# Block sums of a message-passing layer as two 64-column products, and the general path in a branch of its own

## The chip, the cores and the metric

The kernel runs on one core of a Trainium2 chip. The metric is the device time of one execution in microseconds (us), read as the median of several runs. The engines are named as in the profile: PE (TensorE, matrix products), PEld (its weight loads), DVE (VectorE), ACT (ScalarE), POOL (GpSimd, which issues the gathers) and SP (SyncE, which issues plain DMAs).

## The reference

A PaiNN layer on a graph of 1250 nodes with 512 features and 40000 edges that are sorted by their end node `dst`, then a residual and a layer norm. Cut to what matters here:

```python
x_j = x[src]                                  # a gather: 40000 rows
s_j = silu(x_j[:, 384:] @ W1 + b1) @ W3 + b3
split = s_j * (rbf(r) * cutoff(r) @ W2 + b2)
v_msg = v_j * s1 + s3 * edge_attr             # 384 columns
x = x + segment_sum(concat([v_msg, s2]), dst) # first round of sums
row = node_update(x)                          # U, V, Wu1, Wu2: a row for each node
x = x + segment_sum(row[src], dst)            # second round of sums
out = layernorm(x0 + x)
```

## The kernel before, in words

**Tiling.** The sorted edges are cut into 79 chunks of 512 (`CHUNK`), the last of them not full. Four chunks make a group (`CPG`), so there are 20 groups (`NGR`), and two groups feed one block of 128 nodes, so there are 10 blocks (`NB`). The chunk with number c is expected to end in a window of 32 places (`WIN`) that begins 16c - 8 nodes in; neighbouring windows overlap by half, since a chunk's own share is 16 nodes (`SHARE`). If any edge lies outside its chunk's window, the count `misses_v` is not zero and the whole work is done by another function, `general`, in place of `windowed`. With these inputs the count is zero and `windowed` runs. The choice stands at L383 to L387 as an `If` with an `Else`.

**A step.** `windowed` walks over 80 batches t, four to a group; a batch is 4 tiles of 128 edges, one from each chunk of the group. A batch's work:
- `gather` (L745, POOL): four indirect DMAs bring the 128 rows of 640 values of each tile, three batches ahead.
- `edge_factors` (L854, PE): four products make `eb`, the factors of each edge, in four PSUM banks that exist once.
- `messages` (DVE): `hot` (L812, one-hot rows of the place in the window, 32 wide), two multiplications of the gathered rows by `eb` (L865, L869), `pair` (L883) and `spread` (L823). All of them read `eb` or come before the last one that does, so the next `edge_factors` waits for L869.
- `add_messages` (L900, L907, PE): products with `hot` and `spread` as weights of 32 columns add the messages into the PSUM tile `agg`. The four chunks of a group use the four quarters of `agg`: 128 rows, 32 for each chunk. `count_links` (L925) adds up in `adj` which sources each place has, for the second round. `agg` and `adj` exist once.

**Closing a group.** After a group's fourth batch `close_group` (L933 to L956, ACT) copies `agg` to SBUF and makes `high` (L949) and `both` (L951) of `adj`; DVE then does L960 with `both`. An even group goes whole, 128 rows, into the tile `sums_0`. An odd group goes with its first 112 rows (`KEPT`) into its tile `sums_1`, and its last 32 rows are copied once more, to the same rows of the tile of the next odd group (L956). Rows 112 to 127 of an odd group's tile so hold what the odd group before it found for places of this block, and its own last 16 rows stand in the next one's tile alone. Group 1's tile begins with zeros there.

**A block.** `sum_block` (L992, PE) adds the two groups of a block up: `sel` has two matrices of 128 x 128 with a one where a row of the tile belongs to a place of the block (L274), and two products with them add into one PSUM tile, first the even group's and then the odd's. `take_block` (DVE, L1008) adds the nodes' values. The block's node update follows in small pieces on all engines over the next ten steps, among them `turn_nodes` (L1031), `times_u` (L1042), its copy `vu` to SBUF (L1051, ACT) and `times_uv` (L1058, PE). These pieces share one PSUM bank, `work`, so `times_uv` waits until `vu` has been copied out. In the last blocks' steps PE also begins the second round of sums (L1248, `begun`).

**What orders the work.** The order is written out by hand (manual schedule): lists of tasks by step and rank, run at four places of a step. In each step DVE's messages are issued first, then the tasks of `first`, then `add_messages` and `count_links` of the batch before, the tasks of `early`, `edge_factors` of the next batch, a gather, the tasks of `late`, and those of `dve`. Each engine runs its own instructions in that order. Even groups close in step 8b + 4 and odd ones in step 8b + 8 (b from 0). The `vu` copy of the block before falls into the same step as the closing of an even group and stands behind it.

Of the kernel before, what the change touches and what calls it, by code (L numbers as in the profile page):

```python
# [11 lines left out]
F32 = mybir.dt.float32  # L12
# [5 lines left out]
ALU = mybir.AluOpType  # L18
# [3 lines left out]
P = 128  # L22
# [18 lines left out]
WIN = SHARE + 2 * MARGIN  # L41
GSPAN = CPG * SHARE
REACH = GSPAN - SHARE + WIN
KEPT = P - 2 * MARGIN
# [20 lines left out]
def gnn_resnorm(  # L65
# [31 lines left out]
    nc = tc.nc  # L97
    n_nodes, width = x.shape
# [4 lines left out]
    NGR = -(-NCH // CPG)  # L103
    NCP = NGR * CPG

    sh = Shared()
# [116 lines left out]
    for i in range(GROUP):  # L223
# [32 lines left out]
    place = front.tile([P, 3], F32)  # L256
# [7 lines left out]
        place[:, 0:1], place[:, 2:3], float(SHARE - WIN) / WIN, part, op0=ALU.mult, op1=ALU.add  # L264
    )
    nc.vector.tensor_scalar(
        place[:, 2:3], place[:, 0:1], float(P - GSPAN), float(-P), op0=ALU.is_ge, op1=ALU.mult
    )
    nc.vector.scalar_tensor_tensor(
        place[:, 1:2], place[:, 0:1], float(GSPAN), place[:, 2:3], op0=ALU.add, op1=ALU.add  # L270
    )
    sh.sel = const.tile([P, 2, P], F32, name="sel")
    for k in range(2):
        nc.vector.tensor_scalar(sh.sel[:, k, :], lane, place[:, k : k + 1], None, op0=ALU.is_equal)  # L274


    local_r = front.tile([NCP, CHUNK], F32)
# [103 lines left out]
    front_scope.close()  # L381

    misses_v = nc.values_load(missed_i[0:1, 0:1], min_val=0, max_val=n_edges)  # L383
    with tc.If(misses_v == 0) as in_windows:
        windowed(tc, sh)
    with in_windows.Else():
        general(tc, sh)  # L387


# [197 lines left out]
def windowed(tc, sh):  # L587
# [62 lines left out]
    with tc.tile_pool(name="msg", bufs=4) as pool, tc.tile_pool(  # L650
# [72 lines left out]
                nc.vector.memset(magic[:, k : k + 1], (MAGIC, -MAGIC)[k])  # L723


        sums = {1: pool.tile([P, width], F32, name="sums_1", bufs=2)}
        nc.gpsimd.memset(sums[1][P - WIN :, :], 0.0)

        def work():
            return ps_work.tile([P, BANK], F32, name="work")  # L730
# [201 lines left out]

        def close_group(g):  # L933
            agg, rows = aggs.pop(g), group_rows(g)
            if g % 2 == 0:
                assert rows == P
                sums[g] = pool.tile([P, width], F32, name="sums_0", bufs=1)
                nc.scalar.copy(sums[g], agg)
            else:
                if rows < KEPT:  # L940
                    assert rows == P - WIN
                    nc.vector.memset(sums[g][rows:KEPT, :], 0.0)
                own = min(rows, KEPT)
                nc.scalar.copy(sums[g][:own, :], agg[:own, :])
# [6 lines left out]
            nc.scalar.activation(both[:, 1], high, AF.Identity, bias=magic[:, 1:2])  # L951
            boths[g] = both
            if g % 2 and g + 2 < NGR:
                assert rows == P
                sums[g + 2] = pool.tile([P, width], F32, name="sums_1", bufs=2)
                nc.scalar.copy(sums[g + 2][P - WIN :, :], agg[P - WIN :, :])  # L956

        def low_counts(g):
            both = boths[g]
# [27 lines left out]
        def sum_block(b, k):  # L987
            if k == 0:
                blks[b] = (
                    work() if b < NB - 1 else ps_sum.tile([P, BANK], F32, name="begun")  # L990
                )
            nc.tensor.matmul(  # L992
                blks[b], sh.sel[:, k, :], sums.pop(2 * b + k), start=(k == 0), stop=(k == 1)
            )

        node_x = pool.tile([P, width], F32, name="node_x", bufs=1)
# [316 lines left out]
        def at(when, step, rank, fn, *args):  # L1313
            when.setdefault(step, []).append((rank, fn, args))
# [562 lines left out]
```

## Time and profile before

| What | Value |
|---|---|
| median of 3 runs | 594.64 us (591.26 to 596.64) |
| the profiled execution's own time | 585.79 us |
| its span, from the first to the last instruction | 583.8 us |
| granted clock of PE over the span | 0.888 |
| busy: PE / PEld / DVE / ACT / POOL | 445.5 / 240.2 / 441.8 / 373.6 / 354.5 us |
| DMA | 126.95 MB at 217 GB/s |

The profile is one execution. A row of the timeline gives a start in us, a length in us, the engine, the source line, the operation, what it writes and reads, the shapes, a count of merged instructions and, in brackets, how long the engine was idle before it and who ended that wait. A row of a group gives the busy time in us and the mean length in ns. A matmul in fp32 stands in the trace as two records. Ends of matmuls are modelled. "issue" is a wait for which the profile shows no cause.

### The profile page before, as it was taken

To read this page: it belongs to the slowest core of one execution; us is meant where nothing else is said; L and a number is where in the kernel's file an instruction comes from. 1 tells how busy PE (TensorE), PEld (TensorE's weight loads), DVE (VectorE), ACT (ScalarE), POOL (GpSimd) and SP (SyncE) were. 2 spreads that over 40 slices of the span, in tenths; PEclk is the share of its full clock that TensorE was granted. 3 is DMA by queue.
4 is the path that set the end of the run, shared out by engine and by line. 5 is a ranking of instruction groups with operands and counts; after the bars stand their busy time and mean duration, and the time that the engine had idled before them with its cause. 6 is when DMAs were issued, how large, how long until landed. Compare 5 with 4: busy or idle time off the path is not lost. (4 is left out here: it accounts for less than half of the span.)

```text
span 583.8 us, 11028 instructions
## 1 busy us (share of the span) xinstructions
PE 445.5 (76%) x4193; PEld 240.2 (41%) x4193; DVE 441.8 (76%) x698; ACT 373.6 (64%) x941; POOL 354.5 (61%) x369
## 2 busy tenths in 40 slices
PE   2845667687777887697888786787777878798894
PEld 1422323344444344334435443443443444353673
DVE  7685867878878777878877777777787777687685
ACT  1455364757677665767776767777667778656455
POOL 7265767656667665656656665666666576643850
PEclk9966986888899777979888889998989899889998
DMA  8766777786777767767877777777777787859514
GB/s 240 257 189 213 200 224 216 210 262 200 216 224 243 228 197 218 214 205 220 253 245 201 253 226 213 233 231 242 220 229 224 218 240 224 241 148 285 210 38 146
DMA packets 38321, 126.95 MB, mean 217 GB/s; under 512 B 6688, under 2 KB 8238, under 8 KB 38258
## 3 DMA queue, kind: packets, MB, share of 16 engines
q0 software_dynamic: 26016, 104.86, 60.5%
q1 hardware_dynamic: 10910, 20.64, 10.2%
q10 hardware_dynamic: 1332, 0.64, 0.4%
q8 instruction: 35, 0.57, 0.4%
q14 instruction: 28, 0.23, 0.1%
HBM read 114.78 MB, written 11.34 MB: 216 GB/s over the span
## 5 line engine op out<-in xcount | busy, mean ns | idle before, releaser
L745 POOL DMA_INDIRECT more<-table,src_i x189 | 189.9, 1005 | 107.3 <-issue 44.0
L745 POOL DMA_INDIRECT nodes<-table,src_i x124 | 126.3, 1019 | 74.0 <-issue 28.3
L854 PE MATMUL eb<-w_sb,basis_t 25*128 25x388 f32 x626 | 83.5, 585 | 76.6 <-issue 42.2
L845 ACT ACTIVATE one<-one,weight,src_f 128x128 f16<-128x128 f16 x313 | 128.5, 482 | 0.5 <-issue 0.2
L835 ACT ACTIVATE one<-number,low 128x128 f16<-128x128 f16 x313 | 99.8, 392 | 8.5 <-PE adj L925 3.3
L812 DVE TENSOR_TENSOR hot<-lane,eb 128x128 f32<-128x128 f32 (+1 forms) x81 | 22.7, 281 | 81.6 <-PE eb L854 44.7
L869 DVE TENSOR_TENSOR more<-more,eb 128x1536 f32<-128x1536 f32 (+2 forms) x49 | 82.6, 1688 | 0.0
L854 PEld LDWEIGHTS eb<-w_sb,basis_t 25*128 25x128 f32 x626 | 27.5, 196 | 99.5 <-issue 58.0
L900 PE MATMUL agg<-more,hot 128*32 128x512 f32 (+1 forms) x378 | 66.0, 752 | 1.2 <-ACT sums L956 1.2
L865 DVE TENSOR_TENSOR more<-more,eb 128x1024 f32<-128x1024 f32 (+2 forms) x49 | 57.5, 1175 | 0.4 <-issue 0.3
L907 PEld LDWEIGHTS agg<-more,spread 128*32 128x32 f32 x1134 | 39.5, 125 | 40.8 <-issue 40.1
L869 DVE TENSOR_TENSOR nodes<-nodes,eb 128x1536 f32<-128x1536 f32 (+1 forms) x32 | 54.2, 1695 | 0.0
L907 PE MATMUL agg<-more,spread 128*32 128x128 f32 x1134 | 47.8, 298 | 0.0
L823 DVE TENSOR_TENSOR spread<-hot,eb 128x384 f32<-128x384 f32 (+1 forms) x81 | 43.0, 532 | 0.0
L925 PE MATMUL adj<-pair,one 128*128 128x160 f16 x313 | 37.9, 243 | 5.0 <-issue 4.9
L900 PE MATMUL agg<-nodes,hot 128*32 128x512 f32 x248 | 38.5, 680 | 2.4 <-ACT sums L956 2.4
L883 DVE TENSOR_TENSOR pair<-number,column 128x640 f16<-128x640 f16 (+1 forms) x81 | 38.5, 476 | 0.0
L805 ACT COPY basis_t<-work 128x512 f32<-128x512 f32 x20 | 11.7, 587 | 41.1 <-PE work L800 21.7
L865 DVE TENSOR_TENSOR nodes<-nodes,eb 128x1024 f32<-128x1024 f32 (+1 forms) x32 | 37.8, 1180 | 0.0
L960 DVE SCALAR_TENSOR_TENSOR both<-both,adj 128x400 f16<-128x400 f16 (+1 forms) x20 | 11.3, 566 | 32.0 <-ACT both L951 21.1
L907 PEld LDWEIGHTS agg<-nodes,spread 128*32 128x32 f32 x744 | 23.6, 116 | 23.1 <-issue 22.9
L925 PEld LDWEIGHTS <-one 128*128 128x128 f16 x313 | 20.8, 100 | 22.1 <-issue 20.7
(258 smaller groups left out, 728.8 us busy)
## 6 DMA issues: line engine op xcount, KB each, us to landing
table<-more SPq DMA_DIRECT2D x10, 320.0 KB
spilled<-begun SPq DMA_DIRECT2D x12, 256.0 KB
more<-table,src_i POOLq DMA_INDIRECT x189
more<-spilled SPq DMA_DIRECT2D x2, 1280.0 KB
resid<-h_t SPq DMA_DIRECT2D x9, 256.0 KB
node_x<-in_x_dram SPq DMA_DIRECT2D x8, 256.0 KB
nodes<-table,src_i POOLq DMA_INDIRECT x124
nodes<-in_x_dram POOLq DMA_DIRECT2D x2, 768.0 KB
```

What stands on the lines that cost most here:

```text
L745: got = nc.gpsimd.indirect_dma_start(out=rows_t[:n, j, :], out_offset=None, in_=sh.table1, in_offset=bass.IndirectOffsetOnAxis(ap=sh.src_i ...
L812: nc.vector.tensor_tensor(hots[t][:m, js, :], lane[:m, None, :WIN].to_broadcast(shape), eb[:m, js, V + 3 : V + 4].to_broadcast(shape), op= ...
L823: nc.vector.tensor_mul(spread[t][:m, js], hots[t][:m, js, None, :].to_broadcast(shape), eb[:m, js, V : V + 3, None].to_broadcast(shape),)
L835: nc.scalar.activation(onehots[t][:, j, :], number[:, :P], AF.Abs, bias=low[:, e : e + 1])
L845: nc.scalar.activation(one, one, AF.Relu, scale=less[:, e : e + 1], bias=worth[:, e : e + 1])
L854: made = nc.tensor.matmul(eb[:, j, : V + CARRY], turned[g][rows, i, :], sh.w2_sb[rows, :], start=True, stop=True,)
L865: nc.vector.tensor_mul(msg[:m, js, V:], msg[:m, js, V:], eb[:m, js, C:V])
L869: nc.vector.tensor_mul(msg[:m, js, :V].rearrange("p t (k c) -> p t k c", k=3), msg[:m, js, :V].rearrange("p t (k c) -> p t k c", k=3), eb[ ...
L883: nc.vector.tensor_tensor(pair[:m, js, :].rearrange("p t (l h) -> p t l h", h=2), number[:m, : PARTS * WIN].rearrange("p (l h) -> p l h", ...
L900: nc.tensor.matmul(agg[j * WIN : (j + 1) * WIN, :], hots[t][:m, j, :], msg[:m, j, :width], start=(i == 0), stop=False, skip_group_check=True,)
L907: nc.tensor.matmul(agg[j * WIN : (j + 1) * WIN, c * C : (c + 1) * C], spread[t][:m, j, c, :], msg[:m, j, width:], start=False, stop=(i == ...
L925: nc.tensor.matmul(to[:, :, at : at + WIN], one[:m, j, :], pair[:m, j, :].rearrange("e (p n) -> e p n", n=WIN), start=(i == 0 and j == js[ ...
```

## The change

It has three parts.

1. **The groups' tiles.** Each group, even or odd, copies its first 112 rows into its own tile, and, after `high` and `both`, its last 32 rows into rows 96 to 127 of the tile of the *next* group (before: odd groups only, and into the tile of the next odd group). The pools for even groups' tiles hold two and for odd groups' tiles one (before: one and two). The zeros go to group 0's tile.
2. **The block's sums.** A group's tile now holds all that belongs to its own 64 places and nothing else. `sel` becomes one matrix of 128 x 64, the same for both groups. The two products write the upper and the lower 64 rows of the block's PSUM tile, each with `start` and `stop`, instead of adding into all 128. Both are listed as tasks of `first` in the step after the odd group's closing (before: the first of them in `late` of the closing step). For the last block the list is as before.
3. **The branches.** `general` stands in an `If` of its own with the opposite condition, in place of the `Else`.

```diff
-    sh.sel = const.tile([P, 2, P], F32, name="sel")
-    for k in range(2):
-        nc.vector.tensor_scalar(sh.sel[:, k, :], lane, place[:, k : k + 1], None, op0=ALU.is_equal)
+    sh.sel = const.tile([P, GSPAN], F32, name="sel")
+    nc.vector.tensor_scalar(sh.sel, lane[:, :GSPAN], place[:, 1:2], None, op0=ALU.is_equal)
...
-    with tc.If(misses_v == 0) as in_windows:
+    with tc.If(misses_v == 0):
         windowed(tc, sh)
-    with in_windows.Else():
+    with tc.If(misses_v != 0):
         general(tc, sh)
...
-        sums = {1: pool.tile([P, width], F32, name="sums_1", bufs=2)}
-        nc.gpsimd.memset(sums[1][P - WIN :, :], 0.0)
+        sums = {}
+
+        def room_for_sums(g):
+            sums[g] = pool.tile([P, width], F32, name=f"sums_{g % 2}", bufs=2 - g % 2)
+            return sums[g][P - WIN :, :]
+
+        nc.gpsimd.memset(room_for_sums(0), 0.0)
...
         def close_group(g):
             agg, rows = aggs.pop(g), group_rows(g)
-            if g % 2 == 0:
-                assert rows == P
-                sums[g] = pool.tile([P, width], F32, name="sums_0", bufs=1)
-                nc.scalar.copy(sums[g], agg)
-            else:
-                if rows < KEPT:
-                    assert rows == P - WIN
-                    nc.vector.memset(sums[g][rows:KEPT, :], 0.0)
-                own = min(rows, KEPT)
-                nc.scalar.copy(sums[g][:own, :], agg[:own, :])
+            if rows < KEPT:
+                assert rows == P - WIN and g == NGR - 1
+                nc.vector.memset(sums[g][rows:KEPT, :], 0.0)
+            own = min(rows, KEPT)
+            nc.scalar.copy(sums[g][:own, :], agg[:own, :])
...
-            if g % 2 and g + 2 < NGR:
+            if g + 1 < NGR:
                 assert rows == P
-                sums[g + 2] = pool.tile([P, width], F32, name="sums_1", bufs=2)
-                nc.scalar.copy(sums[g + 2][P - WIN :, :], agg[P - WIN :, :])
+                nc.scalar.copy(room_for_sums(g + 1), agg[P - WIN :, :])
...
             nc.tensor.matmul(
-                blks[b], sh.sel[:, k, :], sums.pop(2 * b + k), start=(k == 0), stop=(k == 1)
+                blks[b][k * GSPAN : (k + 1) * GSPAN, :], sh.sel, sums.pop(2 * b + k),
+                start=True, stop=True,
             )
...
-                at(late, begin, 1, sum_block, b, 0)
-                at(first, begin + 1, 1, sum_block, b, 1)
+                for k in range(2):
+                    at(first, begin + 1, 1, sum_block, b, k)
```

The order of the built programs shows where this lands. First ACT where group 2, an even one, is closed and block 0 is being updated. Before (`sums` with a number is one group's tile, `one` the sources' marks of `distances` and `mark_sources`):

```order
L835 ACTIVATE one<-number,low 128x128 x4
L938 COPY sums_1079<-agg 128x512
L949 ACTIVATE high<-adj,magic 128x400
L951 ACTIVATE both<-high,magic 128x400
L1051 COPY vu<-work 128x384
L845 ACTIVATE one<-one,weight,src_f 128x128 x4
```

The same place now:

```order
L837 ACTIVATE one<-number,low 128x128 x4
L941 COPY sums_867<-agg 112x512
L946 ACTIVATE high<-adj,magic 128x400
L948 ACTIVATE both<-high,magic 128x400
L952 COPY sums_1084<-agg 32x512
L1048 COPY vu<-work 128x384
L847 ACTIVATE one<-one,weight,src_f 128x128 x4
```

One copy of 32 rows stands between `both` and `vu` now; the first copy has 112 rows in place of 128. This happens at all ten even groups; odd groups have the same instructions as before.

Then PE at block 0's sums. Before:

```order
L925 MATMUL adj<-pair,one 128x5x32
L854 MATMUL eb<-w_sb,basis_t 128x388 x4
L992 MATMUL work<-sums_659,sel 128x512
L992 MATMUL work<-sums_340,sel 128x512
L900 MATMUL agg<-nodes,hot 32x512 x4
```

And now:

```order
L927 MATMUL adj<-pair,one 128x5x32
L856 MATMUL eb<-w_sb,basis_t 128x388 x4
L988 MATMUL work<-sums_339,sel 64x512
L988 MATMUL work<-sums_663,sel 64x512
L902 MATMUL agg<-nodes,hot 32x512 x4
```

The two products stand at the same place of PE's order as before, although their lines in the task lists differ; each has 64 rows of output.

Last POOL where `windowed` begins. Before, with `ISA` an instruction that adds to a gather queue's semaphore, one ahead of each of the first eight gathers (the first three are shown):

```order
L997 MEMSET node_x 128x512
L1873 ISA
L745 DMA more<-table_189,src_i 128x640
L1873 ISA
L745 DMA more<-table_189,src_i 128x640
L1873 ISA
```

And now:

```order
L786 MEMSET basis 128x16x12
L787 MEMSET basis 128x16
L994 MEMSET node_x 128x512
L747 DMA more<-table_188,src_i 128x640 x12
L747 DMA nodes<-table_188,src_i 128x640 x8
```

The eight stand elsewhere now: where `general` is passed over at the end there is one such instruction for all eight semaphores. Each engine there goes through a second comparison and three jumps (from the end of `windowed` over its own empty other side, over `general`, and to the end), where before it made one jump over `general`. SP's part of the passed-over side has eight more waits for semaphores.

More of the change, by code (lines that the diff above doesn't have):

```diff
@@ L266, in gnn_resnorm @@
     nc.vector.tensor_scalar(
-        place[:, 2:3], place[:, 0:1], float(P - GSPAN), float(-P), op0=ALU.is_ge, op1=ALU.mult
+        place[:, 2:3], place[:, 0:1], float(GSPAN), float(-GSPAN), op0=ALU.is_ge, op1=ALU.mult
     )
-    nc.vector.scalar_tensor_tensor(
-        place[:, 1:2], place[:, 0:1], float(GSPAN), place[:, 2:3], op0=ALU.add, op1=ALU.add
-    )
-    sh.sel = const.tile([P, 2, P], F32, name="sel")
-    for k in range(2):
-        nc.vector.tensor_scalar(sh.sel[:, k, :], lane, place[:, k : k + 1], None, op0=ALU.is_equal)
+    nc.vector.tensor_add(place[:, 1:2], place[:, 0:1], place[:, 2:3])
+    sh.sel = const.tile([P, GSPAN], F32, name="sel")
+    nc.vector.tensor_scalar(sh.sel, lane[:, :GSPAN], place[:, 1:2], None, op0=ALU.is_equal)
     local_r = front.tile([NCP, CHUNK], F32)
```

## The prediction

> **What bounds the kernel now.** The chain at the page's end covers only the last 32 us, so I read the page's busy times first, then who waits for whom, and then the timeline of single steps, since the kernel is 80 steps of the same form.
>
> ```profile
> PE 445.5 (76%) x4193; PEld 240.2 (41%) x4193; DVE 441.8 (76%) x698; ACT 373.6 (64%) x941; POOL 354.5 (61%) x369
> ...
> L812 DVE TENSOR_TENSOR hot<-lane,eb 128x128 f32<-128x128 f32 (+1 forms) x81 | 22.7, 281 | 81.6 <-PE eb L854 44.7
> ```
>
> No engine is full. DVE is idle 81.6 us in front of `hot`, the first instruction of a step, about 1.0 us a step, and mostly for PE's `eb`. One ordinary step from the timeline shows why:
>
> ```profile
> 163.57 1.74 DVE L869 TENSOR_TENSOR nodes<-nodes,eb 128x1536 f32<-128x1536 f32 x1
> 165.37 0.93 PE L854 MATMUL eb<-w_sb,basis_t 25*128 25x388 f32 x8 [0.49 <-issue]
> 167.49 0.29 DVE L812 TENSOR_TENSOR hot<-lane,eb 128x128 f32<-128x128 f32 x1 [1.57 <-PE eb L854]
> ```
>
> L869 ends at 165.31, PE begins `eb` 0.06 us later, and `hot` comes at 167.49, 2.18 us after L869. That is a loop through DVE and PE: messages, then `eb`, then messages. PE work costs nothing as long as `eb` can begin right behind L869. The gathers are not in the loop: `hot` waits for PE and not for a DMA. So every edit is priced at the two steps in which a group closes, where ACT comes into the loop.
>
> **Part 1: two products of 64 columns.** By form, the lines of the group view:
>
> ```profile
> L900 PE MATMUL agg<-more,hot 128*32 128x512 f32 x376 | 65.0, 753 | 1.2 <-ACT sums L956 1.2
> ...
> L992 PE MATMUL work<-sums,sel 128*128 128x512 f32 x36 | 24.2, 802 | 0.6 <-ACT sums L944 0.6
> ...
> L956 ACT COPY sums<-agg 32x512 f32<-32x512 f32 x9 | 5.2, 577 | 0.2
> ```
>
> The products with 32 columns run beside each other: 376 records of 753 ns are 283 us in 65.0 us of busy time, 4.4 at once. L992, with 128 columns, has 36 records of 802 ns in 24.2 us, 1.2 at once. So two products of 64 columns should take about half of 24.2 us over nine blocks, 12.1 us less of PE. Whether a step gets shorter depends on what follows. The step in which group 5 closes:
>
> ```profile
> 197.02 1.99 PE L992 MATMUL work<-sums,sel 128*128 128x512 f32 x4
> 197.03 0.58 ACT L944 COPY sums<-agg 112x512 f32<-112x512 f32 x1 [3.33 <-PE adj L925]
> 198.38 0.63 ACT L951 ACTIVATE both<-high,magic 128x400 f16<-128x400 f32 x1
> 199.03 0.58 ACT L956 COPY sums<-agg 32x512 f32<-32x512 f32 x1
> 199.04 0.57 DVE L960 SCALAR_TENSOR_TENSOR both<-both,adj 128x400 f16<-128x400 f16 x1 [2.80 <-ACT both L951]
> 199.53 0.28 DVE L812 TENSOR_TENSOR hot<-lane,eb 128x128 f32<-128x128 f32 x1
> 199.66 1.06 PE L900 MATMUL agg<-nodes,hot 128*32 128x512 f32 x8 [0.66 <-ACT sums L956]
> 201.72 1.74 DVE L869 TENSOR_TENSOR more<-more,eb 128x1536 f32<-128x1536 f32 x1
> 203.52 0.93 PE L854 MATMUL eb<-w_sb,basis_t 25*128 25x388 f32 x8 [1.76 <-issue]
> ```
>
> DVE waits 2.80 us for ACT's chain copy, `high`, `both`, and goes on to `hot` without a wait for PE. PE ends the two products at 199.01 and then waits 0.66 us until ACT has emptied `agg`. Ending them a microsecond earlier only makes that wait longer; then PE is idle 1.76 us more before `eb`, which begins when L869 is done (203.46). So here the gain is zero. It isn't where PE runs at half of its clock; the block with the longest products:
>
> ```profile
> 249.25 3.78 PE L992 MATMUL work<-sums,sel 128*128 128x512 f32 x4
> ...
> 252.18 1.75 DVE L869 TENSOR_TENSOR nodes<-nodes,eb 128x1536 f32<-128x1536 f32 x1
> ...
> 255.71 0.93 PE L854 MATMUL eb<-w_sb,basis_t 25*128 25x388 f32 x8
> 256.71 0.29 DVE L812 TENSOR_TENSOR hot<-lane,eb 128x128 f32<-128x128 f32 x1 [1.54 <-PE eb L854]
> ```
>
> L869 ends at 253.93, so `hot` could come at 256.11 (2.18 us later, as above) and comes at 256.71. Half of 3.78 us covers that: gain 0.6 us. I looked at all nine such steps, and in the other eight `eb` follows L869 within 0.1 us. The term is -0.6 us; its ends are 0 and -12.1 us.
>
> **Part 2: the groups' tiles.** Odd groups keep their instructions. At each of ten even groups ACT gets one more copy of 32 rows, 577 ns by the L956 row; the other copy stays as long with 112 rows as L944 shows (0.58 us). It stands between `both` and `vu`. Group 12 closes so:
>
> ```profile
> 376.29 0.63 ACT L951 ACTIVATE both<-high,magic 128x400 f16<-128x400 f32 x1
> 376.82 0.46 ACT L1051 COPY vu<-work 128x384 f32<-128x384 f32 x1
> 377.33 1.65 PE L1058 MATMUL work<-uv,x_t 128*128 128x128 f32 x6 [1.26 <-ACT vu L1051]
> ...
> 379.71 1.74 DVE L869 TENSOR_TENSOR nodes<-nodes,eb 128x1536 f32<-128x1536 f32 x1
> ...
> 382.16 0.60 PE L800 MATMUL work<-ident,basis 128*128 128x128 f32 x4
> 382.69 1.42 PE L854 MATMUL eb<-w_sb,basis_t 25*128 25x388 f32 x8
> 384.15 0.29 DVE L812 TENSOR_TENSOR hot<-lane,eb 128x128 f32<-128x128 f32 x1 [1.36 <-PE eb L854]
> ```
>
> PE stands at L1058 for `vu`, already 1.26 us. Behind it on PE are a begun sum, `add_messages`, `count_links`, `turn_basis` and `eb`, and none of them waits again: L854 follows L800 at once, 1.24 us after L869 has ended (381.45). So a copy that makes `vu` 0.58 us later makes `hot` 0.58 us later. DVE's L960 isn't delayed, since the copy stands behind `both`. The release of `agg` comes later too, but ahead of `vu`, so it is never the later one. In some blocks PE arrives early enough. Block 1's step:
>
> ```profile
> 175.75 1.75 DVE L869 TENSOR_TENSOR more<-more,eb 128x1536 f32<-128x1536 f32 x1
> ...
> 177.55 0.93 PE L854 MATMUL eb<-w_sb,basis_t 25*128 25x388 f32 x8
> 179.68 0.29 DVE L812 TENSOR_TENSOR hot<-lane,eb 128x128 f32<-128x128 f32 x1 [0.85 <-PE eb L854]
> ```
>
> Here `eb` begins with L869's end (177.50). Begun at 178.13 it would release `hot` 1.0 us later (as from 255.71 to 256.71), at 179.13, and `hot` comes at 179.68 anyway: no cost. The waits view counts the blocks of the first kind:
>
> ```profile
> PE work L1058 <- ACT vu L1051: 9.9, 7, 2.0
> ```
>
> Seven waits for `vu`, one in each of seven blocks; the other two are like block 1, and group 0 closes with no `vu` behind it. So 7 x 0.58 = +4.1 us. Ends: 0 if something hides them all, 10 x 0.58 = +5.8 us.
>
> **Part 3: the branches, and the front.** These rows are from the line views and the timeline:
>
> ```profile
> L384 DVEq COMPARE_BRANCH  x2: 51/53/55, 30.7 to 578.0; - x2
> ```
>
> ```profile
> L1873 POOLq INC_SWDGE_SEM  x8: 328/354/405, 31.5 to 38.8; - x8
> ...
> L1873 DVEq DRAIN  x2: 10/27/44, 581.2 to 583.2; - x2
> ```
>
> ```profile
> 0.73 0.52 POOL L161 MEMSET dst_r<- 16x512 int32 x1 [0.29 <-POOLq L1857]
> ...
> 6.92 0.47 DVE L274 TENSOR_SCALAR sel<-lane,place 128x128 f32<-128x128 f32 x2
> ...
> 35.67 0.95 POOL L745 DMA_INDIRECT more<-table,src_i  x1 [0.30 <-issue]
> ...
> 43.45 0.95 POOL L745 DMA_INDIRECT more<-table,src_i  x1 [0.30 <-issue]
> ```
>
> The one jump over `general` takes DVE from 578.0 to 581.2, 3.2 us. It stays one: the second comparison jumps over `general` in its place. Two short jumps come new, of the kind that every program has at its start between its first and second block; there POOL was idle 0.29 us with that jump and a barrier in it. Two of these are 0.6 us, and eight more waits of SP at some 28 ns 0.2 us: +0.8 us. Ends: +0.2, and two jumps at the long one's price, +6.4 us. The eight queue instructions of 354 ns that go from the first gathers cost nothing where they were: the gather at 35.67 has one ahead of it and a gap of 0.30 us, the one at 43.45 has none and the same gap. Their removal is worth 0, at most 8 x 0.354 = 2.8 us. `sel` with half of the work takes up to 0.4 us off DVE at 6.9 us, long before the first step; I take 0.
>
> [...]
>
> **Sum.** +4.1 + 0.8 - 0.6 = +4.3 us. The profiled execution took 585.79 us with a span of 583.8, so on its own ground 590.1 us. It is 8.85 us below the median of the runs, 594.64, and outside their 591.26 to 596.64; nothing in the terms depends on that, so I put the sum on the median: 598.9, say 599 us, 0.7% slower.
>
> **Rivals.**
> - *The products do pay.* In a closing step the products would hold the loop, if what ACT waits for came out of PE only behind them. One row speaks for it, a closing step in which ACT's copy begins as the first product ends; against it, at 197.03 above the copy begins with the products. It decides if most closing steps hang on PE. Then -12.1 + 4.1 + 0.8 = -7.2: 587 us. [...]
> - *The copies are hidden.* PE makes up for a late `vu` in the next steps. For it: in ordinary steps PE waits for DVE. Against it: the loop is serial, and a late `hot` moves all that follows. +0.8 - 0.6 = +0.2: 595 us.
> - *The short jumps are long.* If a jump stalls the stream of instructions however short it is, SP and DVE pay 3.2 us twice more behind the last row of output: 4.1 + 6.4 - 0.6 = +9.9: 604.5 us. For it: DVE's 3.2 us; against it: the start's 0.29 us. [...]
>
> **How the numbers follow.** I give the forecast 0.55, the hidden copies 0.15, the long jumps 0.22 and the paying products 0.08. What a measurement can tell from no change is about 1%, 5.9 us. The forecast lies inside it, but with all ten copies and the jumps it reaches +6.6, so about 0.13 of its 0.55 counts as slower: slower 0.35, within 1% 0.56 (0.42 + 0.15, less 0.01 to the other side), faster 0.09. The range leaves out the paying products and the far end of the jumps: 589 to 605 us.
>
> **What would show it.** In the profile after: L988's records overlap and PE's idle time before L902 in closing steps grows; a copy of 0.58 us stands between `both` and `vu`, and PE's waits for `vu` (9.9 us) grow by about 4 us; the steps of odd closings keep their length; from the last output to the span's end it takes 1 us more at most. I would be wrong if `hot` follows ever so late `vu` at its old distance, if the odd closings' steps get shorter, or if the end gets longer by more than 2 us.

## The result, and the profile after

| | before | after |
|---|---|---|
| median of 20 runs each | 592.17 us (588.34 to 598.86) | 592.08 us (586.83 to 602.56) |
| profiled execution, its span | 585.79 us, 583.8 us | 586.83 us, 585.0 us |

The ratio is 0.9994, 95% interval 0.9974 to 1.0015: the change made no difference, to within 1.5 us. The forecast was 599 us. The ratios here leave disturbed runs out, so they need not be the quotient of the medians.

First the busy times, from the page of after, and the groups by form:

```profile
PE 435.9 (75%) x4193; PEld 233.6 (40%) x4193; DVE 440.7 (75%) x697; ACT 380.2 (65%) x951; POOL 356.6 (61%) x369
```

```profile
L988 PE MATMUL work<-sums,sel 128*64 128x512 f32 x36 | 17.1, 778 | 2.2 <-ACT sums L941 2.2
L902 PE MATMUL agg<-more,hot 128*32 128x512 f32 x376 | 63.9, 742 | 3.2 <-ACT sums L952 1.9 <-ACT both L948 1.4
L952 ACT COPY sums<-agg 32x512 f32<-32x512 f32 x19 | 11.0, 578 | 0.5
```

The products do run beside each other, though not two by two: 36 records of 778 ns are 28.0 us in 17.1 us of busy time, 1.6 at once (before 1.2, in 24.2 us). PE waits more in front of L902 (3.2 us in the form shown, before 1.2; 5.2 us with the form that reads `nodes`, before 3.6). The ten new copies are there: 19 of 578 ns in place of 9. Group 12's closing, shown of before in the prediction, now reads:

```profile
374.32 0.63 ACT L948 ACTIVATE both<-high,magic 128x400 f16<-128x400 f32 x1
374.97 0.58 ACT L952 COPY sums<-agg 32x512 f32<-32x512 f32 x1
...
375.57 0.48 ACT L1048 COPY vu<-work 128x384 f32<-128x384 f32 x1
...
376.10 1.65 PE L1055 MATMUL work<-uv,x_t 128*128 128x128 f32 x6 [2.06 <-ACT vu L1048]
...
377.70 1.74 DVE L871 TENSOR_TENSOR nodes<-nodes,eb 128x1536 f32<-128x1536 f32 x1
...
381.28 0.93 PE L856 MATMUL eb<-w_sb,basis_t 25*128 25x388 f32 x8
...
382.28 0.29 DVE L814 TENSOR_TENSOR hot<-lane,eb 128x128 f32<-128x128 f32 x1 [1.51 <-PE eb L856]
```

This is the forecast step: the copy stands ahead of `vu`, PE waits 2.06 us for it (before 1.26), and `eb` begins 1.84 us after L871's end (379.44) where it was 1.24 us. `hot` comes only 0.14 us later than before, 2.84 us after L871 in place of 2.70, since it follows the start of `eb` by 1.00 us here and by 1.46 us there. The waits view, as engine and tile waited for, total, count and longest:

```profile
PE work L1055 <- ACT vu L1048: 12.6, 7, 2.1
...
PE work L1055 <- ACT sums L952: 1.1, 1, 1.1
```

13.7 us, before 9.9: +3.8 us, and about 4 were forecast. Something else must have given the cost back. Two places differ that the forecast did not have. One is the end. SP's last output issues in the timeline, of before and of after:

```profile
578.59 0.74 SPq L1303 DMA_DIRECT2D out_dram<-h_t  x2
```

```profile
577.50 0.74 SPq L1300 DMA_DIRECT2D out_dram<-h_t  x2
```

And what SP does behind them, in the line views of after (shortest, median and longest duration in ns, then the first and the last start):

```profile
L383 SPq COMPARE_BRANCH  x1: 50/50/50, 578.5 to 578.5; - x1
...
L383 SPq EVENT_SEMAPHORE  x8: 17/17/17, 581.2 to 581.7; - x8
...
L1870 SPq EVENT_SEMAPHORE  x14: 17/28/28, 581.8 to 585.0; - x14
```

From the end of the last issue to the end of the span it took 4.43 us (579.33 to 583.76), and takes 6.78 (578.24 to 585.02). The short jump costs 0.2 us, the long one 2.64 us as before (2.68), the eight waits 0.6 us, and behind SP's second closing wait (L1870, at 581.9) comes a gap of 1.6 us that before did not have. In all the end is 2.35 us longer.

The other place is in no view of the order, and shows in the steps. I split the steps in which no group closes or has just closed by half: from step 10 to 35 (14 of them) a step took 6.15 us before and takes 6.17; from 42 to 71 (16 of them) it took 6.33 and takes 6.19. The waits of `hot` hint at it. Before, 23.5 of its 81.6 us of idle time were ended while PE was already at `begun`:

```profile
DVE hot L812 <- PE begun L1248: 23.5, 16, 2.1
```

After, they are 9.4 of 83.8 us:

```profile
L814 DVE TENSOR_TENSOR hot<-lane,eb 128x128 f32<-128x128 f32 (+1 forms) x81 | 22.8, 282 | 83.8 <-PE eb L856 56.8 <-PE begun L1245 9.4 <-PE work L1100 7.5
```

`hot` waits for nothing of `begun`; it was released later than PE's own records, whose ends are modelled, say.

The trace also keeps each update of a semaphore. PE's are about 3 a step in the first half of both kernels. From step 40 on they are 24.8 a step before and 3.1 after. The built programs say why: of the 2405 PE instructions of `windowed` (weight loads and bare waits not counted), 1359 signal before (they add to PE's semaphore) and 276 after, nearly all of the difference in the second half. With the `Else`, the waits of `general` count on the same semaphores, and the signals of consecutive products there aren't merged into one; with two `If`s they are. So part 3 of the change, which I took for a few jumps, also rewrote who signals in `windowed`.

### The profile page after: what moved, and what is told of

Same layout as the page of the kernel before. It is cut to its first block, busy times and chain, and to the rows that moved or that the text cites. A ratio compares the mean times of both kernels' runs of the same rounds, so it can differ in the third digit from the quotient of the medians.

```text
span 585.0 us, 11042 instructions
## 1 busy us (share of the span) xinstructions
PE 435.9 (75%) x4193; PEld 233.6 (40%) x4193; DVE 440.7 (75%) x697; ACT 380.2 (65%) x951; POOL 356.6 (61%) x369
## 4 chain that ended last, share of the span: by engine, by line
PE 48%; DVE 32%; ACT 8%; issue 8%; another core or an unknown queue 2%; DVEq 0%; ACTq 0%
PE eb L856 16%; PE agg L902 8%; DVE more L871 7%; PE agg L909 5%; DVE more L867 5%; DVE nodes L871 4%; DVE spread L825 3%; DVE pair L885 3%; DVE nodes L867 3%; PE adj L927 2%; PE work L1055 2%; PE begun L1245 2%; ACT both L948 2%; PE work L802 1%
## 5 line engine op out<-in xcount | busy, mean ns | idle before, releaser
L814 DVE TENSOR_TENSOR hot<-lane,eb 128x128 f32<-128x128 f32 (+1 forms) x81 | 22.8, 282 | 83.8 <-PE eb L856 56.8
L871 DVE TENSOR_TENSOR more<-more,eb 128x1536 f32<-128x1536 f32 (+2 forms) x49 | 82.7, 1690 | 0.0
L902 PE MATMUL agg<-more,hot 128*32 128x512 f32 (+1 forms) x378 | 64.9, 741 | 3.2 <-ACT sums L952 1.9
L871 DVE TENSOR_TENSOR nodes<-nodes,eb 128x1536 f32<-128x1536 f32 (+1 forms) x32 | 54.3, 1698 | 0.0
L909 PEld LDWEIGHTS agg<-more,spread 128*32 128x32 f32 x1134 | 37.7, 121 | 40.3 <-issue 39.8
L909 PE MATMUL agg<-more,spread 128*32 128x128 f32 x1134 | 46.0, 291 | 0.0
L902 PE MATMUL agg<-nodes,hot 128*32 128x512 f32 x248 | 40.5, 706 | 2.0 <-ACT sums L952 2.0
L941 ACT COPY sums<-agg 112x512 f32<-112x512 f32 (+1 forms) x20 | 11.7, 586 | 46.1 <-remote 22.2
L885 DVE TENSOR_TENSOR pair<-number,column 128x640 f16<-128x640 f16 (+1 forms) x81 | 38.4, 475 | 0.0
L909 PEld LDWEIGHTS agg<-nodes,spread 128*32 128x32 f32 x744 | 25.1, 120 | 23.6 <-issue 23.0
```

The source lines that it names most:

```text
L814: nc.vector.tensor_tensor(hots[t][:m, js, :], lane[:m, None, :WIN].to_broadcast(shape), eb[:m, js, V + 3 : V + 4].to_broadcast(shape), op= ...
L871: nc.vector.tensor_mul(msg[:m, js, :V].rearrange("p t (k c) -> p t k c", k=3), msg[:m, js, :V].rearrange("p t (k c) -> p t k c", k=3), eb[ ...
L885: nc.vector.tensor_tensor(pair[:m, js, :].rearrange("p t (l h) -> p t l h", h=2), number[:m, : PARTS * WIN].rearrange("p (l h) -> p l h", ...
L902: nc.tensor.matmul(agg[j * WIN : (j + 1) * WIN, :], hots[t][:m, j, :], msg[:m, j, :width], start=(i == 0), stop=False, skip_group_check=True,)
L909: nc.tensor.matmul(agg[j * WIN : (j + 1) * WIN, c * C : (c + 1) * C], spread[t][:m, j, c, :], msg[:m, j, width:], start=False, stop=(i == ...
```

## The experiments

Four theories. **A**: the copies cost what the mechanism says, and the branches give it back because PE signals less. **B**: the copies are hidden, and the branches cost their end. **C**: the narrow products pay for the copies. **D**: the branches gain, but by something else than signals. The experiments ran on four chips. On three of them the kernel before takes 584 to 594 us, and on one, used twice, 499 to 500. The two kinds are kept apart below.

**1. The branches alone** (twice, on chips of 585 us):

```diff
 (the kernel before)
-    with tc.If(misses_v == 0) as in_windows:
+    with tc.If(misses_v == 0):
         windowed(tc, sh)
-    with in_windows.Else():
+    with tc.If(misses_v != 0):
         general(tc, sh)
```

> The kernel before with part 3 of the change alone: the general path in an If of its own. Theory A (signals): with the Else, the waits of the general path keep nearly every count of PE's and DVE's semaphores apart in the second half of the windowed path, so 1359 of its 2405 PE instructions signal; with two Ifs 276 do, the update bursts ahead of a release go away, and a step from 300 us on gets 0.1 to 0.3 us shorter: about 40 steps, -4 to -8 us, and the end gets 2.4 us longer. Expected 587 to 590.5 us on 592.2 (ratio 0.991 to 0.997), with late ordinary steps of 6.2 us against 6.33. Theory B (copies hidden, signals worth nothing): +2.4 us for the end, ratio 1.004. Theory C (the products pay for the copies, signals worth nothing): the same, 1.004.

> The kernel before with the two Ifs alone, once more on the chip of the products of 128 columns. On a chip that takes 580 us or more: 0.985 to 0.995 (measured there: 0.983 to 0.995). On a chip of 500 us: 0.993 to 1.000.

Measured 0.9889 (0.9827 to 0.995) and 0.9919 (0.9884 to 0.9954), that is -6.5 us and -4.7 us, though the end is longer by 2.0 to 2.4 us. The first is even more than A's 0.991 to 0.997. B and C, which both say 1.004, fall. Steps without a closing: 6.08 us early and 6.11 late in the first, 6.07 and 6.17 in the second.

**2. The tiles and products alone**, the mirror of it (the changed kernel with the `If` and `Else` of before):

> The changed kernel with the If and Else of before: parts 1 and 2 alone, the tiles and the products of 64 columns. PE signals 1359 times again. Theory A: the copies cost 0.6 us in each of five to seven blocks and nothing pays for them: +3 to +5 us, ratio 1.005 to 1.008, late ordinary steps of 6.33 us as before. Theory B (copies hidden): 1.000 or, as the changed kernel's end of +2.4 us is gone, at most 2.4 us under it: 0.996 to 1.000. Theory C (products pay): 0.996.

> The tiles and products alone, with If and Else. On a chip that takes 580 us or more: 1.006 to 1.016, as measured there. On a chip of 500 us PE isn't waited for (hot waits 20 us in all, and L1058 hardly stands for vu), so the copy of 32 rows should be hidden: 0.998 to 1.002 if so, 1.006 or more if ACT or DVE is held by it there too.

Measured 1.0125 (1.0061 to 1.0189) and 1.0143 (1.01 to 1.0185), on 585 and 594 us: +7.3 us (3.6 to 11) and +8.5 us (5.9 to 11). Both are more than the 1.005 to 1.008 that A said at first. B and C fall again. The two parts are each of a measurable size and of opposite sign. Their middles sum to +1 to +4 us, the whole change measured -0.4 us (-1.5 to +0.9), within what the intervals allow.

**3. Whose signals.** The kernel before with other bodies in its `Else`; all leave out the general path, which isn't run with these inputs:

```diff
     with in_windows.Else():
-        general(tc, sh)
+        nc.vector.memset(sh.xt[:, 0, :], 0.0)        # short Else
...
+        for _ in range(1200):                        # PE's values
+            one = q.tile([P, 128], F32, name="one_p")
+            nc.tensor.matmul(one, sh.ident, sh.ident, start=True, stop=True)
+            nc.scalar.copy(a.tile([P, 128], F32, name="one_s"), one)
...
+        for _ in range(1200):                        # DVE's values
+            one = a.tile([P, 128], F32, name="one_d")
+            nc.vector.memset(one, 0.0)
+            nc.scalar.copy(a.tile([P, 128], F32, name="one_s"), one)
```

Short `Else`:

> The kernel before, with If and Else as they were, but one memset of 64 KB in the Else instead of the general path, which this kernel leaves out (with these inputs it isn't run). No count of the windowed path is kept apart by the other side: 276 of its PE and 363 of its DVE instructions signal. Theory A (signals): the gain of the two Ifs without their longer end, ratio 0.982 to 0.988; late ordinary steps near 6.1 us. Rival D (the two Ifs gain by something of their own, such as where the code lies or the jumps, and not by the signals): this kernel has neither, 0.997 to 1.000, late ordinary steps of 6.33 us.

> The kernel with the short Else again (the general path is left out), because the chip of its first run took 499 us for the kernel before, with 20 us of waits ahead of hot in place of 82: DVE is the bound there and not PE's way to eb. On a chip that takes 580 us or more, theory A: 0.982 to 0.988, late ordinary steps near 6.1 us; rival D: 0.994 to 1.000 (0 to 3 us for the shorter end), late steps 6.33. On a chip like that of the first run: 0.990 to 0.995, as measured there.

PE's values:

> As the kernel with the short Else, but the Else holds 1200 small products of PE, each followed by an ACT copy that waits for it; the general path is left out again. This keeps every count of PE's semaphore in the second half (1333 PE instructions signal, 240 in each tenth from the middle on) and of ACT's, and leaves DVE's merged as with the short Else. Theory A1 (PE's signals cost): late steps as before, 6.3 us, ratio 0.996 to 1.002. A2 (DVE's signals cost): as the short Else, 0.982 to 0.988. D: 0.997 to 1.000.

> The Else with 1200 products and ACT copies again (the general path is left out); PE signals 1333 times. On a chip that takes 580 us or more: if PE's signals cost, late ordinary steps as in the kernel before, 6.3 us, and all of the short Else's gain but its shorter end goes: 0.994 to 1.000; if they don't, 0.982 to 0.988. On a chip like that of the first run: 0.990 to 0.995.

> The Else with 1200 products and ACT copies (the general path is left out), PE signalling 1333 times. On a chip that takes 580 us or more for the kernel before: if PE's signals cost, late ordinary steps 6.3 us and a ratio of 0.994 to 1.000; if they don't, 6.1 us and 0.982 to 0.988. On a chip of 500 us: eb to hot 1.07 us in late steps, 0.992 to 0.995, as in its two runs there.

DVE's values:

> The mirror of it: the Else holds 1200 memsets of DVE, each followed by an ACT copy that waits for it; the general path is left out. All 647 DVE instructions signal, ACT's as in the kernel with the products, and PE's 276 as with the short Else. Theory A1 (PE's signals cost): 0.982 to 0.988, late ordinary steps near 6.1 us. A2 (DVE's): 0.996 to 1.002, 6.3 us. D: 0.997 to 1.000.

> The Else with 1200 memsets and ACT copies again (the general path is left out); DVE signals 647 times. On a chip that takes 580 us or more: if PE's signals cost and DVE's don't, 0.982 to 0.988 and late ordinary steps near 6.1 us; if DVE's cost, 0.994 to 1.000 and 6.3 us. On a chip like that of the first run: 0.993 to 0.999.

> The Else with 1200 memsets and ACT copies (the general path is left out), DVE signalling 647 times and PE 276 times. On a chip that takes 580 us or more: if PE's signals cost and DVE's don't, late ordinary steps 6.1 us and 0.982 to 0.988; if DVE's cost, 6.3 us and 0.994 to 1.000. On a chip of 500 us: eb to hot 1.00 us throughout, 0.993 to 0.997.

And the two `If`s beside them:

> The kernel before with the two Ifs alone again, beside the three with other Else sides on the same chip. On a chip that takes 580 us or more: 0.986 to 0.993, 2 to 4 us over the short Else by its end. On a chip where DVE is the bound, merged signals pay less than the end costs: 1.000 to 1.006.

On a chip of 594 us, PE's values gave 0.9948 (0.9915 to 0.9981) and DVE's 0.9887 (0.9831 to 0.9943). Both have the same short end (2.97 and 2.88 us behind the last issue, before 4.43). The first is within what A said, the second just above it, and the ratios' intervals overlap a little. The traces show where the two part: from step 40 to 72 the one takes 209.4 us and the other 201.7, while from 8 to 40 they take 202.9 and 202.1. `hot` in the two, first with PE's values:

```profile
L816 DVE TENSOR_TENSOR hot<-lane,eb 128x128 f32<-128x128 f32 (+1 forms) x81 | 22.6, 280 | 83.7 <-PE eb L858 46.2 <-PE begun L1252 17.8 <-PE work L1121 5.6
```

```profile
L816 DVE TENSOR_TENSOR hot<-lane,eb 128x128 f32<-128x128 f32 (+1 forms) x81 | 22.7, 281 | 80.4 <-PE eb L858 53.6 <-PE work L1107 9.2 <-PE work L1121 6.9
```

The waits that end at `begun` come back with PE's signals, and not with DVE's (6.8 us), though DVE signals 647 times there. This table sets the profiled executions beside each other. Steps are those without a closing; updates are PE's, a step, from step 40 to 72; the last columns are the unbroken run of updates, under 60 ns apart, that ends ahead of `hot` (how many, and how long; mean of steps 42 to 71):

```
                      PE signals  step early/late  late-early  updates  run of   lasts us
chips of 585 to 594 us
before                   1359       6.15 / 6.33      +0.18      24.8     8.8      0.31
tiles alone              1359       6.08 / 6.34      +0.26      25.2     7.0      0.24
tiles alone, 2nd         1359       6.24 / 6.43      +0.19      24.9     6.6      0.22
PE's values              1333       6.16 / 6.53      +0.37      24.9     8.4      0.29
after                     276       6.17 / 6.19      +0.02       3.1     1.0      0
branches alone            276       6.08 / 6.11      +0.03       3.1     1.0      0
branches alone, 2nd       276       6.07 / 6.17      +0.10       3.0     1.0      0
DVE's values              275       6.19 / 6.24      +0.05       3.0     1.0      0
late copy, 2nd            276       6.15 / 6.26      +0.11       3.0     1.0      0
wide products             276       6.09 / 6.18      +0.09       3.0     1.0      0
chip of 500 us
PE's values              1333       5.21 / 5.31      +0.10      26.1     3.8      0.12
DVE's values              275       5.10 / 5.09      -0.01       3.2     1.0      0
```

On the slower chips, all kernels with 1333 signals or more have a late step that is longer than the early one by 0.18 to 0.37 us, and those with 275 or 276 by 0.02 to 0.11 (the first run of the late copy and the doubled products, not in the table, by -0.04 and -0.10). The granted clock isn't behind it. In the ordinary steps whose mean granted clock was above 0.97, the late ones are longer by 0.25 to 0.28 us in the four kernels with many signals and by at most 0.07 us in the eight with few. The run of updates ahead of `hot`, 0.22 to 0.31 us, is of that size. Some 40 steps from the middle on at about 0.18 us (the means' difference) make 7 us; the branches alone gained 4.7 to 6.5 with 2.0 to 2.4 us lost at the end, so 7 to 9 in the steps. D falls there: the two kernels of the chip of 594 us have the same jumps. In a program built with an `If` inside the `Else`, `windowed` signals 1359 times again (that one wasn't run).

On the chip of 500 us the merged signals hardly pay: the short `Else` gave 0.992 and 0.9854, PE's values 0.9921 and 0.994, DVE's 0.9967 and 0.993, the two `If`s 0.9965 (0.9934 to 0.9995), with half-widths of 0.003 to 0.005. All gain a little, but PE's values are not apart from DVE's. In late ordinary steps `eb` to `hot` takes 1.07 us with PE's values and 1.00 us with the others. Over 40 steps 0.07 us would be 3 us, about what these intervals can tell. The first expectations of the three `Else` sides were written for the slower chips and don't fit: 0.992 and 0.9921 lie in no theory's range, and 0.9967 in that of DVE's signals. Of the later ones, those for PE's and DVE's values held, and two missed: the short `Else` (0.990 to 0.995 said, 0.9854 in the second run) and the two `If`s (1.000 to 1.006 said). The short `Else` was never run on a slower chip.

**4. The late copy.** The changed kernel, with the even groups' copy taken out of `close_group` and put behind `vu`:

```diff
             boths[g] = both
+            if g % 2:
+                hand_on(g, agg)
+            else:
+                left[g] = agg
+
+        left = {}
+
+        def hand_on(g, agg=None):
             if g + 1 < NGR:
-                assert rows == P
+                assert group_rows(g) == P
+                agg = left.pop(g) if agg is None else agg
                 nc.scalar.copy(room_for_sums(g + 1), agg[P - WIN :, :])
...
             at(early, end, 0, close_group, g)
+            if g % 2 == 0:
+                at(early, end, 2, hand_on, g)
```

> The changed kernel with the even groups' copy of 32 rows placed behind vu on ACT instead of between both and vu; odd groups as in the change. Theory A: PE gets vu 0.58 us earlier in the blocks in which it waits for it, and agg still comes free before PE needs it: -2.5 to -4 us against the changed kernel, ratio to the kernel before 0.993 to 0.996. Theory B (copies hidden where they are): no difference to the changed kernel, 1.000. Theory C (the copies cost, the products pay): as A, 0.993 to 0.996.

> The changed kernel with the even groups' copy behind vu. On a chip that takes 580 us or more: 0.983 to 0.991, as measured there. On a chip of 500 us: as the two Ifs alone, 0.994 to 0.999, since the copy's place can't matter where vu isn't waited for.

Measured 0.9868 (0.9829 to 0.9907) and 0.9826 (0.9781 to 0.9871). The changed kernel's interval ends at 0.9974, so this version beats both, by some 1.3 to 1.7%; the gain over the change, 7 us or more, is larger than A's 2.5 to 4 us, and about as large as what the tiles cost alone (7.3 and 8.5 us). Its row of waits and its closing of group 12, in the second of these runs:

```profile
PE work L1064 <- ACT vu L1057: 9.4, 6, 2.1
```

```profile
373.55 0.63 ACT L948 ACTIVATE both<-high,magic 128x400 f16<-128x400 f32 x1
374.09 0.46 ACT L1057 COPY vu<-work 128x384 f32<-128x384 f32 x1
...
374.57 0.58 ACT L961 COPY sums<-agg 32x512 f32<-32x512 f32 x1
374.60 0.94 PE L1064 MATMUL work<-uv,x_t 128*128 128x128 f32 x6 [2.03 <-ACT vu L1057]
...
375.93 1.07 PE L902 MATMUL agg<-more,hot 128*32 128x512 f32 x8
```

`vu` follows `both` again, PE's waits for it are back at 9.4 us, and the copy lies beside L1064: L902, which needs `agg` empty, doesn't wait in this step. Both runs fell on chips of 585 to 594 us, so whether its place matters on the other kind wasn't measured.

**5. The products.** The changed kernel with each narrow product issued twice, and with wide products (`sel` with two matrices of 128 columns, zeros in the other group's half, adding up in one tile):

```diff
 (the wide products; the lines that make `sel` are left out)
...
-            nc.tensor.matmul(
-                blks[b][k * GSPAN : (k + 1) * GSPAN, :], sh.sel, sums.pop(2 * b + k),
-                start=True, stop=True,
-            )
+            nc.tensor.matmul(
+                blks[b], sh.sel[:, k, :], sums.pop(2 * b + k), start=(k == 0), stop=(k == 1)
+            )
```

> The changed kernel with each of the block's products of 64 columns issued twice, so 18 products more in the steps behind odd closings; the sums stay what they are. Theory A: PE waits there for ACT and DVE in any case, so a block's two extra products lie beside that: 0 to +1.5 us, ratio to the kernel before 1.000 to 1.003. Theory B: the same. Theory C (the length of the products holds the step): +9 x 0.8 us and more, ratio 1.012 or above.

> The changed kernel with its tiles, tasks and branches, but with products of 128 columns as before the change: sel holds two matrices again, each with zeros in the other group's 64 columns, and the two products add up in the block's tile. If PE's time in those steps is hidden (theory A, and the prediction's term of -0.6 us): the ratio of the changed kernel, 0.997 to 1.003, with about 12 us more of busy PE. If the narrow products pay for the copies (theory C): 1.008 or above.

Doubled: 1.0004 (0.995 to 1.0058), like the changed kernel's 0.9994. Their rows, doubled and wide:

```profile
L990 PE MATMUL work<-sums,sel 128*64 128x512 f32 x72 | 24.6, 674 | 0.0
```

```profile
L993 PE MATMUL work<-sums,sel 128*128 128x512 f32 x36 | 22.6, 759 | 0.0
```

The first adds 7.5 us of busy PE to the 17.1 and costs nothing that can be measured. The wide ones add 5.5 us and gave 1.006 (1.0011 to 1.0108), 3.9 us over the changed kernel. Neither expectation fits: hidden would be at most 1.003, paying for the copies at least 1.008. The two experiments agree only at their intervals' ends. So the narrow products are worth 0 to some 7 us; which of it stays open, and the step means (those with the products 5.46 us wide and 5.51 narrow) show no place for it. Another pair on record speaks for little: on the same chip the late copy, with tiles and narrow products, took 0.9868 and the branches alone 0.9889. So with the copy out of the way, tiles and products together are worth 1 us, give or take 4.

**6. The general path first**, on the late copy, on a chip of 500 us:

```diff
-    with tc.If(misses_v == 0):
-        windowed(tc, sh)
     with tc.If(misses_v != 0):
         general(tc, sh)
+    with tc.If(misses_v == 0):
+        windowed(tc, sh)
```

> The kernel with the late copy, and the If of the general path ahead of the If of the windowed one, so that the jump over the general path lies at 31 us instead of the end. Theory A: the end gets 2.4 us or more shorter, and the first gathers, which wait for nothing else there, start up to 3 us later; the sum lies between -2.4 us and +0.6 us against the late copy, ratio 0.983 to 0.988. Rival (a jump at the front also delays POOL's table loads and SP's, or code has to be fetched that was held): slower than the late copy by 1 us or more, 0.989 to 0.993.

1.0097 (1.006 to 1.0133): slower, as the rival said, and by more. The late copy itself wasn't run on this chip; the two `If`s alone gave 0.9965 there, so the expected ratios, which go by the slower chips, don't carry over. The end shrinks to 3.33 us, but at the front three engines stand idle until after 33 us:

```profile
33.66 0.33 POOL L652 IOTA number<- 128x256 f16 x1 [14.39 <-DVEq L381]
33.71 1.30 PE L300 MATMUL tp<-ident,counts 80*128 80x80 f32 x8 [7.21 <-DVEq L381]
...
36.43 0.45 DVE L678 TENSOR_SCALAR ratio<-weight 128x320 f32<-128x320 f32 x1 [7.12 <-DMA node_x<-in_x_dram]
...
46.56 0.29 DVE L814 TENSOR_TENSOR hot<-lane,eb 128x128 f32<-128x128 f32 x1
```

The jump over `general` takes DVE from 30.01 to 33.33 us, and the ends of their waits (DVEq L381) say that POOL and PE wait for DVE to come out of it. The first `hot` comes at 46.56 us, where the seven other runs on that chip have it at 38.4 to 42.3. At the end the jump lies beside the landing of the last output for most of its time (in after, SP's ends at 581.17 and the last landing is at 580.33), and at the front it delays all that follows.

## Why the prediction was wrong

**Part 3 is the step that failed.** "It stays one: the second comparison jumps over `general` in its place. Two short jumps come new" counted the instructions that a branch issues, gave +0.8 us, and its ends, +0.2 to +6.4 us, left out a gain. Measured alone it is -4.7 and -6.5 us. An `If` with an `Else` binds the two sides here: the waits on one decide which signals the other keeps (1359 of PE's instructions in `windowed` with `general` in the `Else`, 1333 with PE's values there, 275 with DVE's), and no row of the order shows a signal. The trace of before had it, in the step that is 0.18 us longer in the second half and in the 23.5 us of `hot`'s idle time ended at `begun`, which I did not follow. The traces show PE's updates in rows of 7 to 9 on average, about 40 ns apart, ahead of `hot`; those of 8.4 to 8.8 last 0.29 to 0.31 us. And `hot` begins 23 to 25 ns behind the last of PE's updates in 15 of the 16 late ordinary steps of before, and in 14 of the 16 of after.

Within part 3 the short jumps were rightly ranked (0.2 us, so not long), and the end was still undersized: +2.0 to +2.4 us in all kernels whose second `If` is that of `general`, which was one of the signs of being wrong that I gave. Of it 1.3 to 1.6 us is a gap behind SP's second closing wait. No run here shows its cause.

**Part 2 was right in its mechanism and small in its size.** The copy delays `vu`, `vu` delays `times_uv`, and `eb` with it. "So 7 x 0.58 = +4.1 us" assumed that two of nine blocks hide it and the others pass on just the copy. In the eight steps behind the closings of groups 2 to 16, it takes from the end of the messages to `eb` 1.10 us on average in five runs without the copy there (before, the branches alone and the two `Else` sides; 0.82 to 1.18), 1.75 us in four with it (after 1.41, tiles alone 1.60 and 2.38, wide products 1.60), and 0.64 and 1.18 us in the two of the late copy. That is 0.65 us in each of eight; the step itself gets longer by 0.42 us (6.54 to 6.96), 3.4 us in eight. Behind the closing of group 18, the ninth, the cost takes a way that the prediction didn't have: `eb` follows the messages at once, but DVE waits longer for `square`, which comes from `times_uv`. Before, and after:

```profile
529.67 0.55 DVE L1079 TENSOR_REDUCE s<-square 128x128 f32<-128x384 f32 x1 [2.87 <-ACT square L1062]
```

```profile
528.38 0.55 DVE L1076 TENSOR_REDUCE s<-square 128x128 f32<-128x384 f32 x1 [4.23 <-ACT square L1059]
```

That step takes 7.77 us on average without the copy and 8.99 us with it, so the nine steps together are 4.6 us longer. Timed, the tiles with their products cost 7.3 and 8.5 us, above the end of 5.8 us that I gave; what beyond the steps makes the difference isn't shown.

**Part 1** was sized at -0.6 us; what it is worth stays open between 0 and about -7. The products' busy time fell by 7.1 us, not by the 12.1 us of half of 24.2, since only 1.6 of them run at once. The odd closings kept their length, as forecast: 7.34 and 7.36 us, and the steps behind them 5.49 and 5.51.

**The rivals.** That the products pay, that the copies are hidden and that the short jumps are long are all refuted as the main cause. The time came out nearest to that of the hidden copies, 595 us, for another reason: two parts of 5 to 8 us that cancel. That 592.08 us lies between the 589 and 605 us given is luck.

## What to carry to other kernels

A change of control flow is not only its jumps: look in the built program at which instructions signal, on all engines, since two sides of one branch can share semaphores and one side's waits can stop the other's signals from being merged (here 1359 of PE's signals stayed with the `Else`, and 276 with two `If`s). When steps of the same form have different lengths in two halves of a trace, find out why before pricing a change. A change with several parts that moves nothing should be run part by part, since here a part that gained 1% hid one that lost 1.3%, and moving one copy behind the instruction that is waited for kept the gain (0.9868 and 0.9826).

## What the runs showed of the hardware

The same kernel took 584 to 594 us on some chips and 500 us on another, and it isn't bound by the same engine there. The kernel with DVE's values, on the slower kind and then on the faster one, each with the line of busy times and a step of the timeline:

```profile
PE 443.2 (77%) x4193; PEld 240.0 (41%) x4193; DVE 440.6 (76%) x698; ACT 373.2 (64%) x941; POOL 355.4 (61%) x369
```

```profile
355.78 0.29 DVE L816 TENSOR_TENSOR hot<-lane,eb 128x128 f32<-128x128 f32 x1 [1.02 <-PE begun L1252]
357.98 1.75 DVE L873 TENSOR_TENSOR more<-more,eb 128x1536 f32<-128x1536 f32 x1
359.78 0.93 PE L858 MATMUL eb<-w_sb,basis_t 25*128 25x388 f32 x8 [1.22 <-DVE more L873]
361.99 0.29 DVE L816 TENSOR_TENSOR hot<-lane,eb 128x128 f32<-128x128 f32 x1 [1.27 <-PE eb L858]
```

```profile
PE 400.5 (82%) x4193; PEld 222.3 (45%) x4193; DVE 442.3 (90%) x698; ACT 369.6 (75%) x941; POOL 341.9 (70%) x369
```

```profile
352.14 1.75 DVE L873 TENSOR_TENSOR more<-more,eb 128x1536 f32<-128x1536 f32 x1
353.95 0.94 PE L858 MATMUL eb<-w_sb,basis_t 25*128 25x388 f32 x8 [0.19 <-DVE more L873]
354.95 0.29 DVE L816 TENSOR_TENSOR hot<-lane,eb 128x128 f32<-128x128 f32 x1
```

DVE does the same work in the same time, 440.6 and 442.3 us. But `eb` to `hot` takes 2.21 us on the one and 1.00 us on the other, with the same modelled 0.93 us for the products; the mean granted clock was 0.891 and 0.962. The granted clock of the step doesn't explain it: in the early ordinary steps whose mean granted clock was above 0.97, `eb` to `hot` still takes 2.02 to 2.17 us on the slower chips, and 1.00 to 1.02 us on the faster one. On the slower chips 1.00 us is also seen (381.28 to 382.28 in after), so the products can be done in that time there too. The prediction took 2.18 us for a step's fixed distance; it isn't fixed, and the modelled length of the products, 0.93 us in all these rows, doesn't show what fills it. What makes the chips differ, no run here shows.
